# Layer 1 of a graph network on Trainium2: the scan's silus side by side, exponential and logarithm from one table set, and fewer, wider products

## The chip, the cores and the metric

The kernel runs on one core of one Trainium2 chip. The metric is the device time of one execution in microseconds (us); lower is better. The core has a matrix engine (PE, with PEld for its weight loads), a vector engine (DVE), a scalar engine (ACT) that evaluates functions such as exponential or silu from tables that it loads, a general engine (POOL) and SP, which issues transfers. Each engine works through its own instructions in a fixed order, and waits where data made by another engine is missing.

## The reference, cut to what matters

A network of two layers on `x` of shape (32, 512, 256) with an adjacency `adj` of shape (32, 512, 512). Each layer is a graph step and a feed-forward step on normalized rows, each added to `x`. The change lies in layer 1, whose feed-forward step compresses each batch of 512 rows into 64 "slice" tokens, runs a two-way state-space scan (`_hydra`) over these, and expands again:

```
z, xBC, dt = split(u @ in_w.T)                  # z 512, x 512, B 64, C 64, dt 8 + 8 columns
dt  = softplus(dt + dt_bias)                    # one half forward, one half backward
xBC = silu(causal_conv(xBC, width 3) + conv_b)  # -> x, B, C
dA  = exp(dt * -exp(A_log))
y   = scan(dA, dt, B, x; C), forward + backward
y   = y + x * (x @ fcD_w.T + D)
yg  = y * silu(z)
return (yg * rsqrt(mean(yg**2) + 1e-5) * norm_w) @ out_w.T
```

The graph step of layer 1 is an attention over 4 heads whose weights are masked by `adj`.

## The kernel before

`tile_kernel` runs `layer0_sorted` and then `layer1_plain` (a fallback behind `tc.If` does not run here). The start of layer 1 (its constants, its weights turned by PE) is woven into the end of layer 0. The program is written as generators, and a scheduler then fixes the order of the instructions on each engine; each engine keeps that order.

In `layer1_plain` the 32 batches pass two streams. `attentions` runs `prepare(b)`, `attention(b)` and `norm(b)` for one batch after another. `mixer(g)` takes two batches (`GB = 2`) through `slices` (twice), `tokens`, `scan` and `unslice` (twice); so there are 16 scans. The main loop advances the attention stream by credits while it draws from `mixer`, so that attention work for later batches fills the engines during a scan.

In `prepare`, rows of `x` are gathered by POOL (L1142, indirect transfers), normalized (`normed`: DVE statistics, POOL power, ACT L1121), transposed into `x3T`, and multiplied by the head weights (`hp`, L1171); ACT evaluates three small exponentials of each product (L1174 to L1176) and copies the rest to `ht` (L1177). A Square of the mask with an accumulated sum (L1164) counts its entries; its elementwise result is not needed, and it is written into `ht` before the copies come. A row `mine` is turned, written to DRAM (`ownd`, L1188) and read back to all partitions (`own`, L1191); the attention weights `att` (L1204) need it. `add_rows` (L947) lets POOL's queue add a constant row to `x` by an accumulating transfer.

`scan(g, uT)` works on 128 rows, 64 tokens of each of two batches. In its order:

- `xp` (L1394): x in columns, 16 products; `bcp` (L1403): B and C one after the other, each 64 partitions wide, both on partitions 0 to 63.
- `dtp` (L1422): step sizes laid out for forward and backward in 16 small products, and once more in rows (L1387 with 16 columns).
- the softplus of the step sizes: DVE rows, an exponential (L1431) and a logarithm (L1437).
- `zp` (L1387, 512 columns) and its silu (L1444); convolutions of x (L1411, L1413) and their four silus (L1449); the convolutions of B and of C and their silus (L1456).
- `la`, `seg` (L1475), `gp` (L1481), `segp` (L1485), the exponential `decay` (L1487), `xtp`, `qp`, and the DVE rows `mix` (L1502 to L1504).
- `yp` (L1511): 16 products of 64x64, eight on the upper half of the array for the first batch, then eight on the lower half for the second.
- `y`, its transpose `yTp`, its mean square `ms` (L1524), `oTp` (L1529), `msp` (L1537, four products that spread `ms`), `rms`, `vp` (L1551).

ACT holds one table set at a time. Where the next function is not in it, a load stands before the instruction: in a scan before L1449 (twice), L1431, L1437, L1444 and L1487. PSUM tiles come from one pool (`psum`), each of one bank.

Of the kernel before, what the change touches and what calls it, by code (L numbers as in the profile page):

```python
# [8 lines left out]
F32 = mybir.dt.float32  # L9
# [10 lines left out]
P = 128  # L20
# [844 lines left out]
def layer1_plain(tc, ident, eps, x2s, ranks, adj, w, out, over, ps):  # L865
# [6 lines left out]
    GB = 2  # L872
# [28 lines left out]
    with ExitStack() as ctx:  # L901
# [55 lines left out]
        nc.vector.tensor_scalar_mul(bfx_eps, bfx[:, :, 0], -1e-5)  # L957
        conv_w = const("conv_w", [P, KC, KW], w["hy_conv_w"][:DI].rearrange("(c p) k -> p c k", p=P))
        conv_b = const("conv_b", [P, KC], w["hy_conv_b"][:DI].rearrange("(c p) -> p c", p=P))
        bc_w = const("bc_w", [S, 2, KW], w["hy_conv_w"][DI:].rearrange("(c p) k -> p c k", p=S))  # L960
        bc_b = const("bc_b", [S, 2], w["hy_conv_b"][DI:].rearrange("(c p) -> p c", p=S))
        skip = const("skip", [P, H], w["hy_D"].partition_broadcast(P))
        dtb = ctile("dtb", [P, 4, H])
        for i in range(4):
            nc.sync.dma_start(dtb[:, i, :], w["hy_dt_bias"].partition_broadcast(P))
        nega = const("nega", [P, H], w["hy_A_log"].partition_broadcast(P))
        nc.scalar.activation(nega, nega, AF.Exp)
# [29 lines left out]
        with tc.tile_pool(name="raw", bufs=2, side="right") as raw:  # L997
# [4 lines left out]
            for i in range(2):  # L1002
# [4 lines left out]
            nc.sync.dma_start(bs, w["b_slice"].rearrange("(o n) -> o n", o=1))  # L1007


            pieces = [(dst, w[name], r0)  # L1010
                      for dst, name in ((wfxT, "W_fx"), (inT, "hy_in_w"), (hoT, "hy_out_w"), (owT, "out_w"),
                                        (fcT, "hy_fcD_w"))
                      for r0 in range(0, w[name].shape[0], P)]

            def fetch(i):

# [89 lines left out]

        xs, ready, attended, stored = {}, {}, set(), set()

        def normed(xt, xn, name):

            mv = sb.tile([P, NT, 2], F32, tag="mv" + name[0], name=f"mv{name}")
            for t in range(NT):
                st = sb.tile([P, 6], F32, tag="st" + name[0], name=f"st{name}_{t}", bufs=4)
                nc.vector.bn_stats(st, xt[:, t, :])
                nc.vector.bn_aggr(mv[:, t, :], st)
            rs = sb.tile([P, NT], F32, tag="rs" + name[0], name=f"rs{name}")
            deviation(nc, rs, mv[:, :, 1], eps)
            shift = sb.tile([P, NT], F32, tag="shift" + name[0], name=f"shift{name}")
            nc.vector.scalar_tensor_tensor(shift, mv[:, :, 0], -1.0, rs, ALU.mult, ALU.mult)
            for t in range(NT):  # L1120
                nc.scalar.activation(xn[:, t, :], xt[:, t, :], AF.Identity, bias=shift[:, t : t + 1],  # L1121
                                     scale=rs[:, t : t + 1])
# [13 lines left out]
        def prepare(b):  # L1136
# [12 lines left out]
            if b:  # L1149
# [11 lines left out]


            ht = sb.tile([P, NT, AH * HO], F32, tag="ht", name=f"ht{b}")
            nc.scalar.activation(ht.rearrange("p t e -> p (t e)").bitcast(BF16), mask.rearrange("p t n -> p (t n)"),  # L1164
                                 AF.Square, bias=centre, accum_out=edges[:, b : b + 1])
            other = sb.tile([P, NT, AH], F32, tag="other", name=f"other{b}")
            mine = sb.tile([P, AH, NT], F32, tag="mine", name=f"mine{b}")
            for t in range(NT):
                ph = psum("any", f"hp{b}_{t}")
                for c in range(DC):  # L1170
                    nc.tensor.matmul(ph[:, : AH * (HO + 2)], xnT[:, c, t * P : (t + 1) * P], wa[:, c, :],  # L1171
                                     start=c == 0, stop=c == DC - 1)
                d = ph[:, AH * HO : AH * HO + AH]
                nc.scalar.activation(mine[:, :, t], ph[:, AH * (HO + 1) : AH * (HO + 2)], AF.Exp, scale=1.0 - SLOPE)  # L1174
                nc.scalar.activation(hv[:, t, :, HO], d, AF.Exp)
                nc.scalar.activation(other[:, t, :], d, AF.Exp, scale=SLOPE - 1.0)  # L1176
                nc.scalar.copy(ht[:, t, :], ph[:, : AH * HO])  # L1177
                yield

            nc.gpsimd.tensor_add(hv[:, :, :, :HO], ht.rearrange("p t (h e) -> p t h e", h=AH),  # L1180
                                 abias.rearrange("p (h e) -> p h e", h=AH).unsqueeze(1).to_broadcast([P, NT, AH, HO]))
# [195 lines left out]
        def scan(g, uT):  # L1377
# [13 lines left out]
            px = psum("any", f"xp{g}")  # L1391
            for k in range(KC):
                for c in range(KC):
                    nc.tensor.matmul(px[:, k * T : (k + 1) * T], inT[:, c, DI + k * P : DI + (k + 1) * P],  # L1394
                                     uT[:, c, :], start=c == 0, stop=c == KC - 1)
            xpad = sb.tile([P, KC, GB, LP], F32, tag="xpad", name=f"xpad{g}", bufs=1)
            nc.gpsimd.memset(xpad[:, :, :, : KW - 1], 0.0)
            nc.scalar.copy(xpad[:, :, :, KW - 1 :], px.rearrange("p (k j l) -> p k j l", k=KC, j=GB))
            pb = psum("any", f"bcp{g}")
            for i in range(2):  # L1400
                c0 = 2 * DI + i * S
                for c in range(KC):
                    nc.tensor.matmul(pb[:S, i * T : (i + 1) * T], inT[:, c, c0 : c0 + S], uT[:, c, :],  # L1403
                                     start=c == 0, stop=c == KC - 1)
            bpad = sb.tile([S, 2, GB, LP], F32, tag="bpad", name=f"bpad{g}", bufs=1)
            nc.gpsimd.memset(bpad[:, :, :, : KW - 1], 0.0)
            nc.scalar.copy(bpad[:, :, :, KW - 1 :],
                           pb[:S, : 2 * T].rearrange("p (k j l) -> p k j l", k=2, j=GB))

            def conv(src, wts, dst):  # L1410
                nc.vector.tensor_scalar_mul(dst, src[:, :, 0:G], wts[:, 0:1])  # L1411
# [3 lines left out]

            pd = psum("any", f"dtp{g}")
            for j in range(GB):
                for i in range(2):  # L1420
                    for c in range(KC):
                        nc.tensor.matmul(pd[i * G : (i + 1) * G, j * H : (j + 1) * H],  # L1422
                                         uT[:, c, j * G : (j + 1) * G],
                                         inT[:, c, DT0 + i * H : DT0 + (i + 1) * H],
                                         start=c == 0, stop=c == KC - 1)
            tok_matmul(pd[:, 2 * H : 4 * H], DT0, 2 * H)
            sp = sb.tile([P, 5, 4 * H], F32, tag="sp", name=f"sp{g}")
            v, e, u, r, dt = (sp[:, i, :] for i in range(5))
            nc.vector.tensor_add(v, pd[:, : 4 * H], dtb.rearrange("p i h -> p (i h)"))
            nc.vector.scalar_tensor_tensor(e, v, -1.0, v, ALU.mult, ALU.min)  # L1430
            nc.scalar.activation(e, e, AF.Exp)  # L1431

            nc.vector.tensor_scalar_add(u, e, 1.0)
            nc.vector.reciprocal(r, u)
            nc.vector.scalar_tensor_tensor(e, u, -1.0, e, ALU.add, ALU.subtract)
            nc.vector.tensor_mul(e, e, r)
            nc.scalar.activation(u, u, AF.Ln)  # L1437
            nc.vector.tensor_sub(u, u, e)
            nc.vector.scalar_tensor_tensor(dt, v, 0.0, u, ALU.max, ALU.add)

            pz = psum("any", f"zp{g}")
            tok_matmul(pz, 0, DI)
            z = sb.tile([P, DI], F32, tag="z", name=f"z{g}", bufs=1)
            nc.scalar.activation(z, pz, AF.Silu)  # L1444
            xT = inner(f"xT{g}")
            for k in range(KC):
                dst = chunks(xT)[:, k, :]
                conv(xpad[:, k], conv_w[:, k, :], dst.rearrange("p (j l) -> p j l", j=GB))
                nc.scalar.activation(dst, dst, AF.Silu, bias=conv_b[:, k : k + 1])  # L1449
            bcT = sb.tile([S, 2, GB, G], F32, tag="bcT", name=f"bcT{g}", bufs=1)  # L1450
            cpad = sb.tile([S, GB, G + 2], F32, tag="cpad", name=f"cpad{g}", bufs=1)
            nc.gpsimd.memset(cpad[:, :, 0 : G + 2 : G + 1], 0.0)
            for i in range(2):
                conv(bpad[:, i], bc_w[:, i, :], bcT[:, i])
                dst = bcT[:, 0] if i == 0 else cpad[:, :, 1 : G + 1]
                nc.scalar.activation(dst, bcT[:, i], AF.Silu, bias=bc_b[:, i : i + 1])  # L1456

            la = sb.tile([P, GB, H], F32, tag="la", name=f"la{g}")  # L1460
            nc.vector.tensor_mul(la, dt[:, : GB * H].rearrange("p (j h) -> p j h", j=GB),
# [14 lines left out]
            yield 7  # L1476

            pg = psum("any", f"gp{g}")
            for j in range(GB):
                for i in range(2):  # L1480
                    nc.tensor.matmul(pg[j * G : (j + 1) * G, i * G : (i + 1) * G], bcT[:, 0, j, :],  # L1481
                                     cpad[:, j, 2 * i : 2 * i + G], start=True, stop=True)
            pl = psum("any", f"segp{g}")
            for j in reversed(range(GB)):
# [20 lines left out]

            yield 7
            py = psum("any", f"yp{g}")
            for j in range(GB):
                half = slice(j * G, (j + 1) * G)
                for h in range(H):  # L1510
                    nc.tensor.matmul(py[half, h * C : (h + 1) * C], heads(mix)[half, h, :],  # L1511
                                     heads(xk)[half, h, :], start=True, stop=True)
            y = inner(f"y{g}")
# [17 lines left out]
            oT = inner(f"oT{g}")  # L1531
            nc.scalar.copy(oT, po)

            pm = psum("any", f"msp{g}")
            for j in range(GB):
                for i in range(P // C):
                    nc.tensor.matmul(pm[i * G : (i + 1) * G, j : j + 1], ident[:, j * G : (j + 1) * G], ms,  # L1537
                                     start=True, stop=True)
            rms = sb.tile([P, GB], F32, tag="rms", name=f"rms{g}")
            nc.vector.tensor_scalar(rms, pm[:, :GB], 1.0 / DI, LN_EPS, ALU.mult, ALU.add)  # L1540
            nc.gpsimd.tensor_tensor(rms, rms, eps[:, 1:2].to_broadcast([P, GB]), ALU.pow)
            yield 2

# [689 lines left out]
```

## Time and profile before

| what | value |
|---|---|
| three runs | 4292.98, 4299.84, 4306.08 us; median 4299.84 |
| the profiled execution | 4311.61 us; span 4309.8 us |
| busy, whole span | PE 3825.7, PEld 2426.9, DVE 3170.3, ACT 2188.1, POOL 1584.8 us |
| 3500 to 3700 us, in layer 1 | PE 190.19, DVE 145.06, ACT 97.92, POOL 57.66 of 200 us |
| granted PE clock | 0.949 over the span; 0.98 to 1.00 from 2500 to 4100 us |
| first and last `xpad` copy of a scan | 2522.5 and 4247.1 us |
| ACT table loads in the 16 scans | 96, of 1283 ns each |

Busy times are sums over the span, so a share says nothing of which wait ends last at a given place; for that, one reads the chain of waits and the timelines of one stretch. Scans recur every 111 to 118 us between 2519 and 4140 us. The last two have no or little attention work beside them: between 4139.7 and 4241.7 us PE idles 10.5 us, in the 69.3 us after it 13.6 us, and in each of the groups before 3.2 to 6.7 us.

### The profile page before, as it was taken

The page shows a single profiled execution, that of the slowest core. Times are in us where ns is not written, and L with a number is a line of the kernel's source. Part 1 is how long each engine was busy: PE and PEld are TensorE (multiplying, and loading weights), DVE is VectorE, ACT ScalarE, POOL GpSimd, SP SyncE. Part 2 cuts the span into 40 slices and gives each one's busy share as a digit, 9 for nine tenths or more (in the row PEclk, how much of TensorE's full clock was granted, in tenths as well). Part 3 has the DMA queues.
Part 4 walks back from the last instruction along what each step waited for, and adds up shares of the span by engine and source line. Part 5 has one row for each costly group of instructions (what it writes and reads, how often), then busy time and mean ns, then how long its engine had stood idle before and what let it go on. Part 6 is the DMA issues. An engine that isn't in the chain of part 4 may idle for free.

```text
span 4309.8 us, 56063 instructions
## 1 busy us (share of the span) xinstructions
PE 3825.7 (89%) x19799; PEld 2426.9 (56%) x19799; DVE 3170.3 (74%) x6909; ACT 2188.1 (51%) x4308; POOL 1584.8 (37%) x1973
## 2 busy tenths in 40 slices
PE   5567998989989999888999799999999999999997
PEld 4454565565655656555555355555555555555655
DVE  6668887898778987777776677767777776777763
ACT  3344655566555665555665344454444444444533
POOL 2345643565435644355331322222222223322210
PEclk8778999999999999998999899999999999999998
DMA  4547654575445754377552432333233333232210
GB/s 128 162 154 225 199 164 135 174 231 165 150 127 179 227 163 141 111 248 194 152 157 56 97 70 70 72 74 69 69 79 74 79 79 78 65 74 65 59 30 16
DMA packets 313536, 524.04 MB, mean 122 GB/s; under 512 B 104823, under 2 KB 196611, under 8 KB 313244
## 3 DMA queue, kind: packets, MB, share of 16 engines
q0 software_dynamic: 129408, 383.06, 32.0%
q1 hardware_dynamic: 183836, 137.30, 11.0%
q8 instruction: 158, 2.59, 0.2%
q14 instruction: 134, 1.10, 0.1%
HBM read 463.11 MB, written 73.95 MB: 125 GB/s over the span
## 4 chain that ended last, share of the span: by engine, by line
PE 43%; DVE 21%; DMA 10%; issue 8%; POOL 6%; ACT 4%; DVEq 0%; SPq 0%; POOLq 0%; ACTq 0%
PE clsp L623 5%; PE gatep L623 5%; PE po L652 5%; PE yTp L1341 4%; PE avp L1241 3%; DVE att L1204 3%; PE lgp L1329 3%; DVE acc L637 2%; DMA rows<-table,xs 2%; DVE best L599 2%; DMA best<-table,xs 2%; PE adp L1246 2%; DMA x<-x2s,ranks 1%; PE xp L1394 1%; PE hp L1171 1%
## 5 line engine op out<-in xcount | busy, mean ns | idle before, releaser
L623 PE MATMUL clsp<-xnT,wc 128*128 128x512 f32 x1024 | 523.4, 630 | 47.6 <-ACT cls L625 40.8
L623 PE MATMUL gatep<-xnT,wg 128*128 128x512 f32 x1024 | 496.1, 604 | 14.2 <-ACT gate L625 13.6
L652 PE MATMUL po<-wd,acc 128*128 128x256 f32 x2048 | 453.0, 380 | 4.9 <-DVE acc L641 4.0
L652 PEld LDWEIGHTS po<-wd,acc 128*128 128x128 f32 x2048 | 387.1, 190 | 72.6 <-issue 10.8
L1204 DVE SCALAR_TENSOR_TENSOR att<-own,other,mask 128x512 f32<-128x512 f32 x512 | 365.2, 741 | 57.0 <-DMA own<-ownd 56.9
L599 DVE SCALAR_TENSOR_TENSOR best<-rows,xs,best 128x1024 f32<-128x1024 f32 x212 | 271.1, 1281 | 134.3 <-ACT best L593 81.5
L637 DVE SCALAR_TENSOR_TENSOR acc<-past,fld,acc 128x512 f32<-128x512 f32 x448 | 332.6, 745 | 30.6 <-ACT past L636 22.8
L623 PEld LDWEIGHTS gatep<-xnT,wg 128*128 128x128 f32 x1024 | 195.9, 195 | 253.9 <-issue 199.9
L632 ACT ACTIVATE acc<-tz,fld 128x512 f32<-128x512 f32 x256 | 199.0, 778 | 265.5 <-PE tz L630 235.4
L596 POOL DMA_INDIRECT rows<-table,xs x212 | 258.5, 1219 | 204.3 <-DVE best L599 136.8
L636 ACT ACTIVATE past<-tz,fld 128x512 f32<-128x512 f32 x448 | 291.1, 694 | 80.1 <-DVE acc L637 79.7
L623 PEld LDWEIGHTS clsp<-xnT,wc 128*128 128x128 f32 x1024 | 184.3, 201 | 185.1 <-issue 114.7
L1241 PE MATMUL avp<-att,hv 128*32 128x512 f32 x2048 | 257.3, 605 | 30.8 <-DVE att L1204 30.8
L435 PE MATMUL pm<-h,adj 128*128 128x258 f32 (+1 forms) x1024 | 179.6, 322 | 100.5 <-DVE keep L428 39.0
L1341 PE MATMUL yTp<-sw,x 128*128 128x512 f32 x512 | 239.0, 609 | 32.0 <-DVE sw L1336 22.6
L1142 POOL DMA_INDIRECT x<-x2s,ranks x128 | 151.0, 1179 | 309.7 <-DVE x L1563 138.1
L625 ACT ACTIVATE gate<-gatep,fld 128x512 f32<-128x512 f32 x256 | 175.8, 687 | 161.6 <-PE gatep L623 132.6
L1329 PE MATMUL lgp<-wsl,x4T 128*128 128x512 f32 x512 | 244.9, 620 | 13.1 <-ACT x4T L1131 7.2
L1294 POOL TENSOR_TENSOR mu<-mu,eps 128x16 f32<-128x16 f32 x32 | 115.4, 3606 | 371.0 <-DVE mu L1293 371.0
L554 POOL DMA_INDIRECT xs<-rows_of,order x128 | 156.4, 1222 | 253.3 <-DVE acc L637 100.3
L1561 PE MATMUL outp<-v,swT 128*128 128x256 f32 x1024 | 227.4, 380 | 0.0
L435 PEld LDWEIGHTS pm<-h,adj 128*128 128x128 f32 x1024 | 150.2, 211 | 125.8 <-issue 71.3
(585 smaller groups left out, 8393.6 us busy)
## 6 DMA issues: line engine op xcount, KB each, us to landing
adj<-in_adj POOLq DMA_DIRECT2D x128, 256.0 KB
x<-added POOLq DMA_DIRECT2D x64, 512.0 KB
own<-ownd SPq DMA_DIRECT2D x128, 256.0 KB
rows_of<-keep SPq DMA_DIRECT2D x32, 550.0 KB
x<-in_x SPq DMA_DIRECT2D x32, 512.0 KB
xs<-bd POOLq DMA_DIRECT2D x32, 512.0 KB
x2s<-xs SPq DMA_DIRECT2D x32, 512.0 KB
short<-in_adj POOLq DMA_DIRECT2D x32, 512.0 KB
```

The costliest lines, as they stand in the source:

```text
L435: nc.tensor.matmul(pm[:, : c1 - c0], a[:, i, t * P : (t + 1) * P], h[:, i, c0:c1], start=i + c0 == 0, stop=i + 1 == NT and c0 > 0)
L596: nc.gpsimd.indirect_dma_start(out=row, out_offset=None, in_=table, in_offset=bass.IndirectOffsetOnAxis(ap=idxs[:, k : k + 1].bitcast(U32) ...
L599: nc.vector.scalar_tensor_tensor(m, row, vals[:, k : k + 1], m, ALU.add, ALU.max)
L623: nc.tensor.matmul(pf, wf[:, c, f * P : (f + 1) * P], xnT[:, c, :], start=c == 0, stop=c == DC - 1)
L636: nc.scalar.activation(r, z, AF.Relu, bias=fld[:, f, AT + b : AT + b + 1])
L637: nc.vector.scalar_tensor_tensor(y, r, fld[:, f, CH + b : CH + b + 1], y, ALU.mult, ALU.add)
L652: nc.tensor.matmul(po[:, i, :], acc[f][:, t * P : (t + 1) * P], wd[:, f, :], start=f == 0, stop=f == FC - 1)
L1204: nc.vector.scalar_tensor_tensor(e, own[h], other[:, j, h : h + 1], mask[:, j, :], ALU.max, ALU.mult)
L1241: nc.tensor.matmul(pv[p][k * HW : (k + 1) * HW, :], hv[:, j, h, e : e + HW], weighed[b, h, j], **ends)
L1329: nc.tensor.matmul(pf, xnT[:, c, t * P : (t + 1) * P], wsl[:, c, :], start=c == 0, stop=c == DC - 1)
L1341: nc.tensor.matmul(py, xn[:, t, c * P : (c + 1) * P], sw[:, t, :], start=t == 0, stop=t == NT - 1)
L1561: nc.tensor.matmul(po[:, :D], swT[:, k, t * P : (t + 1) * P], v[:, k, :], start=k == 0, stop=k == KC - 1)
```

## The change

It does these things in `layer1_plain`:

- The columns of `in_w` are stored with the 16 step-size columns first, so that they lie beside z. `z` is computed as two products: step sizes with the first half of z (272 columns, into the bank `pb` of B and C), and the second half (256 columns, bank `pz`).
- B and C become one product, one convolution on 128 partitions; the silu of C moves it from partitions 64 to 127 to partitions 0 to 63.
- The small products of the step sizes are gone; five DVE additions arrange the halves from the rows.
- All silus come together; then one set that holds exponential and logarithm is loaded explicitly, and the exponential, the logarithm (and later `decay`) are ordered behind it (`behind`, `tc.issue_after`).
- `gp` and `yp` alternate between the two batches, product by product.
- `msp` is gone; four DVE instructions on 64 partitions spread `ms`.
- The Square of the mask is written into `xnT` (`x3T`), after the `hp` products, no longer into `ht` before them.

```diff
-            nc.scalar.activation(ht.rearrange("p t e -> p (t e)").bitcast(BF16), mask.rearrange("p t n -> p (t n)"),
-                                 AF.Square, bias=centre, accum_out=edges[:, b : b + 1])
...
+            nc.scalar.activation(xnT.rearrange("p c n -> p (c n)").bitcast(BF16), mask.rearrange("p t n -> p (t n)"),
+                                 AF.Square, bias=centre, accum_out=edges[:, b : b + 1])
...
+            pb, pz = psum("any", f"bcp{g}"), psum("any", f"zp{g}")
+            for c in range(KC):
+                nc.tensor.matmul(pb[:, :T], inT[:, c, DIN - P :], uT[:, c, :], start=c == 0, stop=c == KC - 1)
+            first = 2 * H + DI // 2
+            tok_matmul(pb[:, T : T + first], 0, first)
+            tok_matmul(pz[:, : DI // 2], first, DI // 2)
...
+            nc.vector.tensor_add(v[:, 2 * H :], pd, dtb.rearrange("p i h -> p (i h)"))
+            for i in range(2):
+                for j in range(GB):
+                    half = slice(j * G, (j + 1) * G)
+                    nc.vector.tensor_add(v[i * G : (i + 1) * G, j * H : (j + 1) * H],
+                                         pd[half, i * H : (i + 1) * H], dtb[half, 0, :])
...
+            silus.append(nc.scalar.activation(z[:, : DI // 2], pb[:, T + 2 * H : T + first], AF.Silu))
+            silus.append(nc.scalar.activation(z[:, DI // 2 :], pz[:, : DI // 2], AF.Silu))
...
+            conv(bpad, bc_w, bcT)
+            for half, dst in ((slice(0, S), bcT[:S]), (slice(S, P), cpad[:, :, 1 : G + 1])):
+                silus.append(nc.scalar.activation(dst, bcT[half], AF.Silu, bias=bc_b[half]))
+            xT = inner(f"xT{g}")
+            for k in range(KC):
+                dst = chunks(xT)[:, k, :]
+                conv(xpad[:, k], conv_w[:, k, :], dst.rearrange("p (j l) -> p j l", j=GB))
+                silus.append(nc.scalar.activation(dst, dst, AF.Silu, bias=conv_b[:, k : k + 1]))
...
+            both = nc.scalar.preload_act_table_set("natural_log_exp_and_others")
+            for silu in silus:
+                behind(both, silu)
+            with tc.issue_after(both.ins):
+                nc.scalar.activation(e, e, AF.Exp)
...
+            with tc.issue_after(both.ins):
+                nc.scalar.activation(u, u, AF.Ln)
...
-            for j in range(GB):
-                half = slice(j * G, (j + 1) * G)
-                for h in range(H):
+            for h in range(H):
+                for j in range(GB):
+                    half = slice(j * G, (j + 1) * G)
                     nc.tensor.matmul(py[half, h * C : (h + 1) * C], heads(mix)[half, h, :],
                                      heads(xk)[half, h, :], start=True, stop=True)
...
-                    nc.tensor.matmul(pm[i * G : (i + 1) * G, j : j + 1], ident[:, j * G : (j + 1) * G], ms,
-                                     start=True, stop=True)
+                    nc.vector.tensor_scalar(rms[i * G : (i + 1) * G, j : j + 1], ms[j * G : (j + 1) * G], 1.0 / DI, LN_EPS,
+                                            ALU.mult, ALU.add)
```

and the new helper, which orders one instruction behind another on the same engine without a semaphore:

```python
        def behind(ins, other):
            order = mybir.DependencyInfo(mybir.DependencyClass.NoSync, mybir.DependencyReason.DATA)
            tc.add_manual_dep(ins.ins, other.ins.name, order, reason="tables")
```

Two constants shrink with it: `dtb` is filled by two transfers, not four, and the weights of B's and C's convolution are loaded as one block of 128 partitions.

## The prediction

> **What bounds the kernel now.** I read the busy table first (PE 3825.7 us of 4309.8, DVE 3170.3), then the stretches: in layer 1, from 2500 to 4100 us, every 200 us hold 188 to 193 us of PE and only 140 to 149 us of DVE. So PE looks like the bound of the stage that the change touches. Then the chain of waits over one mixer group (two batches, one scan), 3560 to 3680 us; its period, from one `xp` to the next, is 117.0 us, of which PE idles 6.5 us. The columns are start, time, engine and line:
>
> ```profile
> 3562.40 3.77 PE xp L1394 x32
> 3566.17 1.89 PE bcp L1403 x16
> 3568.06 1.20 PE dtp L1422 x32
> 3569.26 0.99 PE dtp L1387 x8
> 3570.25 3.53 PE zp L1387 x8
> ...
> 3579.94 0.39 PE gp L1481 x8
> 3580.32 1.01 PE segp L1485 x4
> ...
> 3590.86 0.26 ACT turned L1186
> 3591.14 6.04 DMA ownd<-turned
> 3597.19 3.31 DMA own<-ownd
> ...
> 3608.65 3.44 DMA out<-x
> ```
>
> The reader is to see two regimes. From `xp` to `segp` the chain is PE without a gap. From `turned` to the softmax products `yTp` (3636.8) it is not PE at all: a row goes to DRAM and back (9.35 us), DVE makes attention weights and adds `x`, `x` is stored, the next `x` is gathered, POOL raises to a power, DVE scales `sw`. A PE saving is kept only in the first regime, and there only if ACT and DVE could have been ready earlier. How ready they were is in the timelines of ACT, of DVE and of PE (start, length, what, and in brackets the idle time before it and its releaser):
>
> ```profile
> 3573.78 1.28 ACT L1437 ACT_TABLE_LOAD   x1
> 3575.13 0.23 ACT L1437 ACTIVATE sp<-sp 128x32 f32<-128x32 f32 x1
> ```
>
> ```profile
> 3568.81 0.48 DVE L1411 TENSOR_SCALAR xT<-xpad,conv_w 128x128 f32<-128x128 f32 x2
> ...
> 3577.94 0.16 DVE L1119 SCALAR_TENSOR_TENSOR shiftd<-mvd,rsd 128x4 f32<-128x4 f32 x1 [1.41 <-POOL rsd L31]
> ```
>
> ```profile
> 3586.19 1.87 PE L1511 MATMUL yp<-xk,mix 64*64 64x64 f32 x32 [0.71 <-DVE mix L1504]
> ...
> 3595.53 3.67 PE L1551 MATMUL vp<-owT,oT 64*64 64x256 f32 x32 [0.34 <-ACT oT L1532]
> ```
>
> DVE reaches the convolutions only at 3568.81, 2 us after `xpad` stood ready, because it first finishes the norm of the batch before; `seg` was ready at 3579.97, 0.3 us before PE came to `segp`. DVE was as late as PE.
>
> **PE work, from start-to-start distances** (x32 is 16 matmuls, two records each). Removed: `bcp` 1.79, the halves of `dtp` 1.29, `dtp` in rows 0.92, `zp` 3.51: 7.51 us. Added: 4 of 128x128 at 3.77/16 = 0.236: 0.94; 4 of 272 columns at 0.46 (`hp`, 264 columns, leaves two every 0.89 us): 1.83; 4 of 256 columns at 0.438 (`outp`: 16 in 7.01): 1.75. Sum 4.52, so 2.99 less. `msp` frees 0.40, but `vp` behind it waits for the copy `oT` anyway: 0.
>
> For `yp` in turns, row and rule differ. The row is `vp`: two 64x64 tiles in turns, 16 matmuls of 256 columns in 3.60 us, 0.225 each, half of `outp`'s 0.438. So `yp` falls from 1.80 to 0.90 us. The Trainium skill ("TensorEngine Tiling (Array Packing)", section Restrictions and Gotchas) says that different row tiles cannot access one PSUM bank at once; `py` is one bank and its two halves are different row tiles, so by the rule `yp` stays at 1.80 (+0.9 us a group on my sum). `vp` writes its halves into one bank too, so I take the row. `gp`, in turns over column strips like `avp`, falls from 0.38 to about 0.2. In all PE has 4.1 us less a group (4.5 with `msp`), 72 us over 16 groups if all were kept.
>
> **ACT: six table loads become two** (the built order shows one before the first silu, one behind the last), 4 x 1.283 = 5.1 us a group. The skill ("ScalarE: Activation LUTs", section What ACT_TABLE_LOAD costs) gives 1.283 us and a drain of 1.38 us, which would make it 10.6 us; the trace agrees on the load and shows no drain (3575.13 follows 3573.78 by 1.35), so 5.1. On the path it is worth little: the old loads ran beside PE's 17.5 us. What is new on the path is the order: exponential, `seg` and `segp` now stand behind all silus.
>
> **Timetable of this group after the change**, by the built order and the durations above. DVE is unchanged to 3568.81. Four convolutions (0.75 each) 3571.85, one `att` 0.66, five step-size adds (0.1 apart; four are new, cross-partition, not in the trace: between 0.06 and 0.19 each, the spacing and the length of `sp` rows; I take 0.1) 3573.0; `bcT` with two batch-norm rows between, 3574.7. It is one convolution of 128 partitions instead of two, 0.75 less. Silus of B and C to 3575.4, load to 3576.7, exponential 3576.95; DVE has waited for `rsd` (1.41) meanwhile. Logarithm behind two `x` rows on ACT, 3578.4; sub, `dt`, `la` 0.22 each, `seg` 1.29: 3580.4. So `segp` starts **0.1 us later** than now (3580.32). PE, earlier by 2.9, waits 1 us for `gp` (the silu of C) and 2 us for `seg`. Its saving is gone here, and with it the cover of the exponential: each us there now costs one.
>
> From `segp` to `yp` nothing changes (`dq` waits for `qp`, then five DVE rows of 0.6): `yp` 3586.3. `yp` halved: y done 0.8 us earlier. But the **Square of the mask** (2.00 us, L1164) moves. Now it stands at the head of `ht`, where it made ACT wait (62.5 us over 27 times, `mu` L1292) and once a group kept exponentials of `sw` behind it (3622.83); PE waited 1.52 us for that. In the new order it follows the fourth `hp` copy, ahead of `yT` and `turned`: copy ends 3588.75, Square 3590.75, `yT` 3591.4. So `oTp` and `vp` come **0.45 later** than now, `turned` 1.2 later. In the second batch it delays two `x4T` copies by 0.5. Queued behind it on ACT are `yT`, the square of y, `turned`; PE waits for the first, DVE through `own` for the last.
>
> Against it: `hv` and `x` (L1121) now run on ACT before `decay`, at 3577 to 3581.4, not 3586 to 3589. POOL's two `x<-added` transfers, 512 KB each, wait for them and start some 7 us earlier. Now they fill the DMA engines from 3588 to 3594.6 (96% busy in 3590 to 3595), in front of `ownd`, which takes 6.05 us; in the second batch, with nothing before it, 1.39. The first batches of the 14 groups lie between 3.1 and 6.1, mostly near 4. After the change: 3592.4 + 1.4 + 3.3 = 3597.1 against 3600.53. DVE's sum of `x` then waits for `outp`, not for `own`: it ends 3607.0 instead of 3608.54, and store, gather, power and `sw` follow 1.5 earlier. In the next group it is 1.1. Minus 0.5 for `x4T`: **about 1.0 us a group gained**. Bounds: 0.5 lost (where `ownd` was fast already) to 3 gained (groups 2 and 3, where `lgp` waits 2.7 us behind the Square).
>
> The last two groups have little attention to fill with. In the last, PE waits 4.36 for `gp`, 3.48 for `yp`; `seg` comes about 2.3 earlier with fewer loads and `yp`, 3.28 there at the lower clock, halves: 4. The one before: `yp` halves, 2. The rest: two SP transfers fewer at the start, beside layer 0's PE, 0; piece order of `inT`, same ten pieces, 0; three small DVE rows for `rms`, 0.3 us beside `oTp`, 0.
>
> **Sum**: 14 x 1.0 + 2 + 4 = 20 us. The profiled execution took 4311.6 (span 4309.8), so 4291.6 like for like; it lies 11.8 over the median 4299.84, so **4280** as a median.
>
> **Rivals.** *PE keeps its saving* (0.16): the DVE chain had slack that I don't see, and the count of PE decides: 14 x 4.4 + 6 = 68, 4232. For it: PE at 95%. Against: `seg` 0.3 us ahead of PE.
> *The silus hold the exponential* (0.21, slower): one mechanism, at L1431. If the convolution of B and C ends later than 3574.7, everything to `segp` shifts by as much, with no cover. The adds at 0.19, a dependent convolution row of 0.34 and one more `att` ahead make 1.5 to 2.5. At 2.5, each group loses 1.5: 14 x 1.5 - 4 = +17, 4317. It decides from 1 us on.
> *The transfers are not relieved* (0.17): `ownd` stays slow beside the transposed mask (3574.4) or the write's own landing; then only the later `turned` is left, +1.3: 14 x 1.3 - 6 = +12, 4312.
> As worked (0.46): 4262 to 4296.
>
> What this kernel can tell from no change is 0.3%, 13 us: below 4287 is faster, above 4313 slower. Faster: 0.40 of the first case and all of the PE rival, 0.56; slower 0.14 of the silu rival and 0.05 of the transfers, 0.19; same 0.25. Leaving out the ends of both rivals, 4236 to 4314.
>
> **What would show it.** Table loads in layer 1 from 96 to 32; `yp` near 0.9 us (right) or 1.8; PE waiting about 1 for `gp` and 2 for `segp` in each group (if neither, the PE rival holds; if over 4, the silu rival); `ownd` to `own` 1.4 in first batches; Square 2.0 just ahead of `yT`, `oTp` waiting over 1.5. I am wrong if PE's idle time a group falls below 6.5, or if the period grows.

## The result and the profile after

The change makes no difference: 14 runs of each gave 4304.39 us (4286.51 to 4310.56) against 4303.49 (4291.78 to 4314.58); the ratio of after to before is 1.0007, 95% interval 0.9993 to 1.002. The forecast was 20 us less. The profiled execution took 4294.7 us (span 4293.0), but it entered the first scan at 2498.9 us, before's at 2518.7. That is layer 0 and not the change: in the 15 profiled executions of this document the first scan begins anywhere between 2496 and 2526 us. From the first scan to the end of the span it is 1791.1 us before and 1794.1 after. So single profiles are compared here by the distance from one `xp` to the next (the period of a group), and kernels by their ratio. A period is of one execution, and a difference of half a us between two says little: three kernels below that differ only in what fills one wait have 115.07, 115.50 and 115.58.

| mean of groups 0 to 13, us behind `xp` | before | after | change |
|---|---|---|---|
| `segp` | 17.65 | 18.29 | +0.64 |
| `yp` | 23.61 | 24.04 | +0.43 |
| `oTp` | 28.43 | 29.39 | +0.96 |
| `vp` | 32.94 | 34.95 | +2.01 |
| next `xp` (the period) | 115.79 | 116.39 | +0.60 |

14 groups lose 8.4 us together, group 14 gains 3.6, the last 1.8. PE is busy 53.5 us less (3772.2 for 3825.7) and ACT 83.1 less (2105.0 for 2188.1), and neither shows in the time.

The timeline of PE in group 9 after (its `xp` starts at 3548.38; columns: start, length, what, and in brackets the idle time before it and its releaser):

```profile
3561.73 0.45 PE L1491 MATMUL gp<-cpad,bcT 64*64 64x64 f32 x8 [1.47 <-ACT cpad L1445]
3562.11 1.92 PE L1248 MATMUL avp<-att,hv 128*32 128x512 f32 x16
3563.85 1.04 PE L1253 MATMUL adp<-att,hv 128*32 128x512 f32 x8
3566.72 1.08 PE L1495 MATMUL segp<-seg,seg_l 128*64 128x512 f32 x4 [1.83 <-DVE seg L1485]
```

```profile
3572.66 1.15 PE L1521 MATMUL yp<-xk,mix 64*64 64x64 f32 x32 [0.71 <-ACT ht L1182]
3573.74 1.16 PE L1176 MATMUL hp<-wa,x3T 128*128 128x264 f32 x4
3575.41 0.63 PE L1531 MATMUL yTp<-ident,y 128*128 128x128 f32 x4 [0.51 <-DVE y L1526]
3575.87 0.27 PE L1191 MATMUL minep<-ident,mine 128*16 128x128 f32 x1
3578.02 5.46 PE L1539 MATMUL oTp<-yT,hoT 128*128 128x128 f32 x32 [1.88 <-ACT yT L1533]
3584.16 2.16 PE L1559 MATMUL vp<-owT,oT 64*64 64x256 f32 x18 [0.68 <-ACT oT L1542]
```

PE waits 1.47 for `gp`, 1.83 for `segp` and 1.88 for `oTp`. In the same group of before it waited for neither of the first two, and 0.62 for `oTp`. `yp` is short (1.08 from its start to that of `hp`). New is the 5.46 of `oTp`; in before the same sixteen products took 3.84:

```profile
3591.01 3.84 PE L1529 MATMUL oTp<-yT,hoT 128*128 128x128 f32 x32 [0.62 <-ACT yT L1523]
```

The next view, the stretches of group 9, shows why (after, columns: stretch, its length, busy time of PE, PEld, DVE, ACT and POOL, the granted clock, DMA share, GB/s):

```profile
3574.00:3576.00 2.00, 1.49 (x9) 0.89 (x8) 1.23 (x2) 1.06 (x5) 0.41 (x1) 1.00 0.00 0
3576.00:3578.00 2.00, 0.14 (x2) 0.00 (x0) 0.04 (x1) 2.00 (x4) 1.93 (x1) 1.00 0.00 0
3578.00:3580.00 2.00, 1.98 (x13) 1.98 (x14) 1.90 (x8) 0.69 (x3) 0.00 (x0) 0.72 0.02 4
3580.00:3582.00 2.00, 2.00 (x11) 2.00 (x11) 0.00 (x0) 0.00 (x0) 0.71 (x1) 0.50 0.26 86
3582.00:3584.00 2.00, 1.48 (x12) 1.29 (x11) 0.54 (x1) 0.48 (x1) 0.00 (x0) 0.92 0.95 314
```

PE stands nearly still for 2 us, then starts at full clock and is cut to half for 3.4 us (the clock records of the trace come in pieces of 3.413 us). Group 7 of the same execution has the same waits and no cut, so the length of the wait alone does not decide. What differs is where it falls. From the first scan on, the 19 low stretches of after all begin on one grid of 3.413 us, to within 1 ns, and this grid lies differently to the program in each execution. One piece of it in group 9, then the three around the start of `oTp` (3348.01) in group 7:

```profile
3575.48:3578.89 3.41, 1.53 (x12) 1.25 (x13) 0.93 (x3) 3.21 (x7) 2.34 (x1) 1.00 0.00 0
3343.37:3346.78 3.41, 2.26 (x24) 1.45 (x20) 1.38 (x2) 1.85 (x5) 1.20 (x1) 1.00 0.03 5
3346.78:3350.20 3.42, 2.19 (x19) 2.19 (x20) 1.93 (x8) 1.90 (x6) 1.33 (x2) 1.00 0.01 2
3350.20:3353.61 3.41, 2.73 (x25) 2.21 (x26) 0.29 (x1) 0.92 (x2) 0.52 (x1) 1.00 0.67 204
```

In group 9 PE idles 1.88 of 3.41 us in one piece, and the next runs at half clock. In group 7 a border of the grid divides the wait, 1.15 and 1.23 us are idle in two pieces, and the clock stays. Nine of the 14 groups are cut (0, 3, 6 and 8 to 13); the piece before the cut holds 1.86 to 2.38 us of idle in them, and in the other five no piece there holds more than 1.50, but for group 2 with 1.86. From `oTp` to `vp` it is 6.14 us in the cut ones, and 4.51 in the other five and in all 14 of before (where no piece holds more than 1.13).

What PE waits for is in the timeline of ACT, same group:

```profile
3575.11 0.39 ACT L1182 COPY ht<-hp 128x256 f32<-128x256 f32 x1
3575.36 2.03 ACT L1184 ACTIVATE x3T<-mask,centre 128x2048 bf16<-128x2048 bf16 x1
3577.27 0.22 ACT L1184 ACTIVATION_READ_ACCUMULATOR x3T<-mask,centre 128x1 f32 x1
3577.36 0.60 ACT L1533 COPY yT<-yTp 128x512 f32<-128x512 f32 x1
```

The Square stands just ahead of `yT`, as the built order had said. The chain of waits now runs from it through `yT`, `oTp`, `vp` and `outp` to DVE's sum of `x`, so the low clock of `oTp` lies on it.

### The profile page after: what moved, and what is told of

Read it like the earlier page. It is cut to its first block, busy times and chain, and to the rows that moved or that the text cites. A ratio compares the mean times of both kernels' runs of the same rounds, so it can differ in the third digit from the quotient of the medians.

```text
span 4293.0 us, 54585 instructions
## 1 busy us (share of the span) xinstructions
PE 3772.2 (88%) x19031; PEld 2392.6 (56%) x19031; DVE 3183.1 (74%) x6973; ACT 2105.0 (49%) x4260; POOL 1576.3 (37%) x1973
```

## Experiments

The questions were: does the low clock cost the time, or only go with it; what in the wait brings it; is the Square's new place the cause; and what is the rest worth, the grouping of tables, the order of softplus and silus, the turns of `yp`. Kernels that ran together share their runs of before. "Period" is the mean of groups 0 to 13 in the one profiled execution, "cut" the number of these groups in which `oTp` ran at the low clock there.

| run | differs from | ratio to before (95%) | period | cut |
|---|---|---|---|---|
| after | | 1.0007 (0.9993 to 1.002) | 116.39 | 9 |
| warm2 | after | 0.9972 (0.9959 to 0.9985) | 115.58 | 0 |
| warm1 | after | 0.9967 (0.9953 to 0.9981) | 115.07 | 0 |
| warm_tr | after | 0.9958 (0.9943 to 0.9974) | 115.50 | 0 |
| sq_turn | after | 0.9970 (0.9958 to 0.9982) | 115.30 | 0 |
| sq_old | after | 0.9960 (0.9947 to 0.9972) | 115.16 | 0 |
| b_sq | before | 1.0009 (0.9996 to 1.0022) | 116.37 | 7 |
| exp_first | sq_old | 0.9927 (0.9909 to 0.9944) | 114.58 | 0 |
| exp_turn | sq_turn | 0.9896 (0.9879 to 0.9914) | 113.59 | 0 |
| exp_new | after | 0.9936 (0.9915 to 0.9958) | 114.85 | 8 |
| no_group | sq_old | 1.0133 (1.0117 to 1.0149) | 119.41 | 4 |
| b_tab | before | 0.9981 (0.9966 to 0.9997) | 115.38 | 0 |
| b_yp | before | 0.9997 (0.9986 to 1.0008) | 115.65 | 0 |
| et_yp | exp_turn | 0.9896 (0.9872 to 0.9920) | 114.06 | 0 |

### The low clock: warm2, warm1, warm_tr

```diff
             po = psum("any", f"oTp{g}")
+            for _ in range(2):      # warm1: range(1)
+                nc.tensor.matmul(po, ident, y, start=True, stop=True)
```

In warm_tr the line is `nc.tensor.transpose` of one 128-column block of `y` into a block of `po`, eight times. What they write, `oTp` overwrites.

> After, plus two matmuls of 128x512 into oTp's bank while PE waits for yT; oTp overwrites what they wrote. Theory A (clock gate): in 9 of 14 groups oTp (16 products) runs at a granted clock of 0.5 and takes 5.46 us instead of 3.84, because PE idles just before it. With PE busy there, oTp starts as late as in after (29.4 us behind xp) but oTp to vp falls from 5.56 to 4.5 in all groups, the period by about 1.0, the time by 10 to 16 us. Theory B (oTp is long for another reason, e.g. PE's operands or ACT's copy oT; or the chain downstream absorbs it): oTp to vp stays near 5.5, or it falls and the period stays at 116.4: time unchanged within 4 us.

> As warm2, with one extra product instead of two: PE's wait for yT (1.88 us in after, 0.15 in warm2) is filled to about half, some 1.0 us remain. If the low clock depends on how much of a stretch PE idles: no group, or few, with the low clock; oTp (extra product counted in) to vp near 5.5 in all groups, oTp starting 0.85 later than in warm2; time within 5 us of warm2. If any wait of a microsecond at this place brings it: groups with 1.6 us more, as in after, and the time near after's.

> As warm1, but PE's wait for yT is filled by eight transposes of 128x128 (by the spacing of yTp 0.12 us each, some 1.0 us) instead of one ordinary product of 1.02 us. Theory A (any work of PE keeps the clock): as warm1, no group with the low clock, oTp proper to vp 4.5, ratio to before 0.996 to 0.998. Theory B (transposes do not count as work: in after the low clock follows 3.12 us without an ordinary product, from the end of hp to oTp, in which yTp and minep, transposes both, ran): the low clock stays in 6 to 11 of 14 groups, and the time is that of after (1.000 to 1.002).

The timeline of PE in group 9 of warm1, and then of warm_tr:

```profile
3566.44 1.02 PE L1539 MATMUL oTp<-y,ident 128*128 128x512 f32 x2
3568.47 3.84 PE L1542 MATMUL oTp<-yT,hoT 128*128 128x128 f32 x32 [1.01 <-ACT yT L1534]
3572.98 2.38 PE L1562 MATMUL vp<-owT,oT 64*64 64x256 f32 x20 [0.68 <-ACT oT L1545]
```

```profile
3598.40 1.04 PE L1539 MATMUL oTp<-ident,y 128*128 128x128 f32 x8
3600.44 3.84 PE L1542 MATMUL oTp<-yT,hoT 128*128 128x128 f32 x32 [1.00 <-ACT yT L1534]
```

`oTp` proper starts no earlier in group 9 than in after (29.65 us behind `xp` in both, 29.64 there) and takes 3.84 again; no group is cut. Work was added to PE, the traces show all other instructions of PE, ACT, DVE and POOL in the order of after, and the ratio fell by 0.0035, 0.0040 and 0.0049 from that of after, 15 to 21 us of 4300. Nine times 1.63 would be 14.7; up to 4.6 us more come from the last group (66.3 us in after, 65.9, 62.7 and 61.7 here). Theory A of warm2 holds: the low clock costs the time. Of warm1's two readings the first holds: half of the wait filled is enough. No piece of the grid before `oTp` then holds more than 1.52 us of idle, so the missing cuts are no luck of the grid. And warm_tr tells that it is PE's standing still: transposes keep the clock as products do.

### The Square's place: sq_turn, sq_old, b_sq

```diff
-            nc.scalar.copy(row, pt[: AH * NT, :P])
+            turned_row = nc.scalar.copy(row, pt[: AH * NT, :P])
+            square = nc.scalar.activation(xnT.rearrange("p c n -> p (c n)").bitcast(BF16),
+                                          mask.rearrange("p t n -> p (t n)"),
+                                          AF.Square, bias=centre, accum_out=edges[:, b : b + 1])
+            behind(square, turned_row)
```

That is sq_turn, with the Square taken from its place in after. sq_old puts it where it was in before; b_sq is before with that one line moved as the change moves it.

> After, with the Square ordered behind the copy of the turned row, so no longer ahead of yT. Theory A (the Square's place costs twice: 0.5 us of wait and the low clock that this wait brings): yp to oTp falls from 5.35 to about 3.5 to 4, oTp to vp from 5.56 to 4.5, vp about 33 us behind xp, ownd issued 1.2 to 2 us earlier; 1.5 to 2 us a group, 20 to 30 us in all: 4274 to 4284 beside 4304 of after. Rival C (the end of a group is set by the attention chain, not by oTp): vp comes earlier but the period falls by less than 0.5; time within 7 us of after.

> After, with the Square back in its old place (into ht, ahead of the head products); all else as in after. If the new place of the Square is what spoilt the change: oTp to vp 4.5 and vp about 33 us behind xp as in sq_turn, but the waits of lgp and mu behind the Square (1 to 2.7 us a group in before) are back: 5 to 15 us under after. If the old place costs as much as the new one: within 5 us of after.

> Before, with only the Square moved (into the transposed rows, behind the head products). If the Square's new place alone brings the late yT and the low clock: yp to oTp over 5.2 and oTp to vp over 5 in most groups, against 4.82 and 4.51 in before; time 5 to 12 us over before, less what lgp no longer waits (1 us a group). If the low clock comes only from the joint effect with a shorter yp and PE's new waits for gp and segp: oTp to vp stays 4.5, the time 0 to 10 us under before.

The line of `oTp` in group 9 of sq_turn, then of b_sq:

```profile
3580.37 3.84 PE L1541 MATMUL oTp<-yT,hoT 128*128 128x128 f32 x32 [0.56 <-ACT yT L1535]
3577.02 5.39 PE L1529 MATMUL oTp<-yT,hoT 128*128 128x128 f32 x32 [1.87 <-ACT yT L1523]
```

Out of its new place, by either way, the Square no longer holds `yT`: `oTp` waits 0.56 us, `oTp` to `vp` is 4.51 in groups 0 to 13, and 16 (sq_turn) and 20 us (sq_old) are won against after. (The scheduler also set other rows of ACT and DVE in a new order in both, so the gain is not the Square's alone.) For sq_turn that is theory A in kind and less than its 20 to 30 us; rival C falls, as the period fell by 1.09. sq_old gained more than expected: waits of `lgp` behind it came back in two groups (2.92 and 4.06 us), not in most. b_sq shows that nothing else of the change is needed: before with the Square moved waits 1.88 at `oTp` and is cut in 7 groups. Its time is not told from before's. Its groups are 0.58 longer in the profile, 8 us in all, which the interval (2 us less to 9 more) allows; the waits for `lgp` (11.3 us over groups 0 to 13 of before) went with the move, but that they pay for the cuts is not shown.

With `segp` at the same place, the period of groups 9 and 10 can be set against `vp`: at 32.86 us (sq_old, sq_turn) it is 114.7 to 114.9, at 34.2 (warm1, warm2, warm_tr) 114.1 to 114.4, at 35.8 (after) 115.9 and 115.95. In these two groups the wait alone, 1.3 us, costs nothing that shows, and the 1.6 of the low clock, which come on top, cost all of 1.6. This is a hint and no proof: each is one execution, and warm2 has 115.7 in groups 7 and 8 without a cut.

### Softplus and silus: exp_first, exp_turn, exp_new, no_group, b_tab

```diff
+            nc.scalar.activation(e, e, AF.Exp)
...
+            ln = nc.scalar.activation(u, u, AF.Ln)
...
             silus = []
...
             both = nc.scalar.preload_act_table_set("natural_log_exp_and_others")
             for silu in silus:
+                behind(silu, ln)
                 behind(both, silu)
-            with tc.issue_after(both.ins):
-                nc.scalar.activation(e, e, AF.Exp)
...
-            with tc.issue_after(both.ins):
-                nc.scalar.activation(u, u, AF.Ln)
```

In exp_first softplus stands in the program ahead of the silus (the diff against sq_old, cut), with the Square in before's place; exp_turn has the Square behind the turned row, exp_new where the change has it. no_group is sq_old with no order between softplus and silus and no explicit load; b_tab is before with exponential and logarithm behind all silus, as in the change, and nothing else.

> As sq_old (after with the Square in its old place), but exponential and logarithm stand ahead of the silus, on the set that is still loaded; the silus are ordered behind the logarithm, the set for exponential and logarithm is loaded again behind the last silu: still two loads a scan. Theory A (the price that ate PE's saving is the place of the exponential: it stood ready 3.4 us and waited for the silus and a load): the wait for seg (1.83 us) and most of that for gp (1.48) go, segp starts 15 to 15.5 us behind xp instead of 18.3, vp near 30; as the gathers meet the next mask's transfer, a third to a half of it is kept: 1 to 1.5 us a group, 14 to 20 us under sq_old. Rival B (the end of a group is set by the attention chain on DVE, POOL and DMA): segp comes earlier, but yp and the period keep their times within 0.4 us; time within 6 us of sq_old.

> As exp_first, with the Square behind the turned row. In after, the same move and the move back to the old place gave nearly the same time (4286.7 and 4285.4). If that holds here too: within 5 us of exp_first. If exp_first makes lgp wait behind the old Square, as before did in five of 14 groups (1 to 2.7 us): 5 to 15 us under exp_first.

> As exp_turn (softplus ahead of the silus), with the Square in the place that the change gave it, ahead of yT. It fills the two by two with after, sq_turn and exp_turn. If the Square's place costs by its wait and by the low clock here too: oTp waits about 1.9 us, oTp to vp 6.1 in half of the groups or more, 10 to 20 us over exp_turn. If the low clock in after needed the waits for gp and seg as well: oTp to vp 4.5 and 3 to 8 us over exp_turn.

> As sq_old, without the grouping of tables: exponential and logarithm in the place and with the loads of before (six loads a scan, about 5.1 us more of ACT). Theory A (the grouping itself costs on the path, since the exponential waits for all silus): segp 1 to 2 us earlier than in sq_old, the time 5 to 15 us under sq_old. Rival B (the loads removed pay for the order): segp as late as in sq_old or later, by up to 2 us, and the last two groups 2 to 4 us longer; time 0 to 20 us over sq_old.

> Before, with the grouping of tables alone: exponential and logarithm behind all silus, loads from six to two a scan; products, Square and yp as in before. Theory A (the loads removed are what the change gains, as taking the grouping out of sq_old cost 71 us): segp no later than in before and 10 to 40 us faster, the last two groups by 2 us each. Rival B (the six loads hurt only with the merged products, where all silus come at once; in before they lay beside PE): segp 0.5 to 2 us later than before's 17.65, since the exponential now waits for the silu of C; 0 to 25 us slower.

First what after does, in the timelines of DVE (first line) and ACT, group 9:

```profile
3559.41 0.18 DVE L1434 SCALAR_TENSOR_TENSOR sp<-sp 128x32 f32<-128x32 f32 x1
```

```profile
3561.28 0.40 ACT L1445 ACTIVATE cpad<-bcT,bc_b 64x128 f32<-64x128 f32 x1
3561.70 1.28 ACT L1455 ACT_TABLE_LOAD   x1
3562.99 0.23 ACT L1459 ACTIVATE sp<-sp 128x32 f32<-128x32 f32 x1
3563.38 1.10 ACT L1128 ACTIVATE x<-x,shiftd,rsd 128x256 f32<-128x256 f32 x2 [0.16 <-DVE shiftd L1126]
3564.38 0.21 ACT L1466 ACTIVATE sp<-sp 128x32 f32<-128x32 f32 x1
```

The exponential's operand is done at 3559.59 and stands 3.40 us, behind the silu of C and a load of 1.28; the logarithm then stands behind two `x` rows. The same stretch of exp_turn (its `xp` at 3538.97), ACT and then PE:

```profile
3548.51 0.23 ACT L1437 ACTIVATE sp<-sp 128x32 f32<-128x32 f32 x1 [2.67 <-DVE sp L1436]
3548.65 0.56 ACT L1138 COPY x3T<-x3T22p 128x512 f32<-128x512 f32 x1
3549.69 0.23 ACT L1443 ACTIVATE sp<-sp 128x32 f32<-128x32 f32 x1 [0.48 <-DVE sp L1441]
3549.94 1.28 ACT L1450 ACT_TABLE_LOAD   x1
3551.24 0.38 ACT L1450 ACTIVATE z<-bcp 128x256 f32<-128x256 f32 x1
```

```profile
3552.64 0.45 PE L1493 MATMUL gp<-cpad,bcT 64*64 64x64 f32 x8 [0.48 <-ACT cpad L1457]
3553.01 1.04 PE L1250 MATMUL avp<-att,hv 128*32 128x512 f32 x2
3553.99 1.08 PE L1497 MATMUL segp<-seg,seg_l 128*64 128x512 f32 x4
```

Here it is ACT that waits for the operand, not the reverse. PE comes to `segp` at 15.02 us without a wait, 3.3 earlier than in after, with the same two loads a scan. Not all of that reaches `yp`: it is 1.0 earlier in exp_first than in sq_old, and 2.3 in exp_turn than in sq_turn. exp_first is 0.0033 below sq_old (14 us, the low end of theory A; its period fell by 0.58 and not by 1 to 1.5, and 5 us came in group 14), exp_turn 0.0074 below sq_turn (32 us): **exp_turn beats both kernels, by 1.0%**. The old place of the Square is worse once the rest is faster (`lgp` waits 3.09 and 3.60 in groups 2 and 3 of exp_first): exp_turn is 13 us under exp_first (six runs of each, and the intervals overlap a little). exp_new, 0.0040 over exp_turn, fills the square: `oTp` waits 1.86 in most groups and 8 are cut (17 us): the first reading. The wait for `seg` is gone there, and 1.07 of that for `gp` is left in the mean; that the cut needs neither is shown by b_sq, which has none of the two.

no_group is far outside what was expected, 74 us over sq_old: rival B has the sign, but it went to 20. Silu, exponential, silu, logarithm, silu and `decay` alternate there, a load before each; PE waits 3.8 us for `gp`, and the mean granted clock from 2500 to 4100 us is 0.96 (0.99 in sq_old, 1.00 in before). How the 74 us divide between these was not tried. b_tab is 8 us faster than before (the interval just clear of none), short of theory A's 10. `segp` was 0.16 later, and PE waited 0.61 for it; the gain is 5.7 us over groups 0 to 13 and as much in group 14, where `yp` waits 1.02 instead of 4.71. So the grouping is worth 8 us in before and 74 with the merged products. That it is so because these let all silus come at once is argued from the order in no_group, not shown by a run.

### The turns of yp: b_yp, et_yp

```diff
-            for j in range(GB):
-                half = slice(j * G, (j + 1) * G)
-                for h in range(H):
+            for h in range(H):
+                for j in range(GB):
+                    half = slice(j * G, (j + 1) * G)
```

> Before, with only the order of yp's products changed (the two batches in turns). By the row of vp, yp falls from 1.87 us busy to about 1.0 to 1.15. Theory A (the saving is kept, since PE and the row sent to DRAM both follow yp): 0.8 us in each of 16 groups: 10 to 14 us under before. Rival B (the row's slow write, not yp, sets the end): time within 4 us of before. If different row tiles of one bank were serialized: yp stays at 1.87 and the time at that of before.

> As exp_turn, with yp's products in the order of before. In before the turns were worth 1.6 us in all (not told from none), since the end of a group did not follow yp there. If PE leads to vp in exp_turn: the eight and eight cost 0.6 to 0.8 us a group, 8 to 13 us over exp_turn. If the attention chain sets the end here as well: within 4 us of exp_turn.

In before the turns are worth nothing that can be told (0.9997): `oTp` comes 0.49 earlier, and the period follows by 0.14 (rival B). In exp_turn the old order has `vp` 0.72 later and the same ratio; the expected 8 to 13 us did not come, though with six runs of each the intervals cannot exclude 8 us, and the period of the one profile is 0.47 longer.

## Why the prediction failed, by its steps

- **The step that failed** is "So `oTp` and `vp` come **0.45 later** than now". `oTp` came 0.96 later (29.64 in group 9 for the forecast 29.1), of which 0.41 stood already at `segp`. But between `oTp` and `vp` the prediction took before's 4.51 for granted, and it became 6.14 in nine groups: the wait in front of `oTp` brings the low clock, a term that it put at nothing. The term is 1.05 us a group, 15 us in all by its own length, and 15 to 21 us by the three runs that took it away. With it removed and all else kept, the change is 0.28 to 0.42% faster, 12 to 18 us, where 20 was forecast. Before's own profile held the warning, and the prediction used it for `yp` alone ("3.28 there at the lower clock"): in groups 14 and 15, where PE waits most, `oTp` to `vp` is 7.21 and 5.89. I saw a new wait of 1.3 us and priced only the wait.
- **The sum "14 x 1.0"** took one group for all, and this failed too. Group 9 did fall by 1.03 (116.98 to 115.95), but that it met the forecast was luck: 1.52 of `lgp` wait had gone, which only eight of the groups had (11.3 us in all), and 1.6 of low clock had come. Over the 14 groups a gain of 14 us was forecast and a loss of 8.4 measured; 14.7 of the difference is the low clock by its own length. Without the cuts the mean period falls by 0.21 (warm2), 0.29 (warm_tr) or 0.72 (warm1), not by 1.0. So the 12 to 18 us of the kernels without cuts come near the forecast in part because the last two groups gain 6 to 10 in them.
- **Silus, load, exponential: right in time.** Times behind `xp` in group 9: the exponential is done at 14.84 (forecast 14.6), the logarithm at 16.21 (16.1), and `segp` begins at 18.34 (18.1). PE waits 1.47 and 1.83, where 1 and 2 were forecast. The silu rival was to decide from 1 us on; it stayed below, +0.64 in the mean, of which 0.23 is group 0 alone (+3.26). Yet its place was the right one to look at: what PE saved was lost there, and turning the order round brings 32 us.
- **PE work, `yp`: right in kind.** `yp` takes 1.08, where 0.90 was forecast; the row of `vp` held, and the rule on row tiles that share a bank, which would have left 1.80, did not. `gp` stayed at 0.38 (forecast 0.2), with no effect, as PE waited in front of it. All of PE's saving was to vanish in waits, and did.
- **Table loads: right.** 32 loads in the 16 scans, 1283 ns each, followed by the next row after 1.29: no drain, as the row said. "Worth little on the path" held in before (8 us by b_tab), not for the merged products (no_group).
- **Transfers: right.** From the issue of `ownd` to that of `own`, 1.36 (3578.71, 3580.07), for 1.4 forecast (1.34 to 1.38 in ten of the 14 groups, 1.68 to 3.50 in the other four); the first `att`, which `own` releases, began 35.08 behind `xp` (34.8). It was not kept, because `outp` then came last, as forecast, but too late (DVE waits 3.59 for it): DVE's sum of `x` ended 47.0 behind `xp` instead of the forecast 44.7, and 2.1 of the difference is `vp` (35.78 for the forecast 33.65).
- **Last groups:** -3.6 and -1.8, forecast -2 and -4; the sum was right.
- **Its signs:** those that it named for its mechanism came (the fast transfer in ten of 14 groups), and so did one of its two signs of being wrong: the period grew.

## What to carry to other kernels

Where a change puts a wait of 1 to 2 us in front of a run of products, add up PE's idle time within 3.4 us there, the waits just before included, and price the products at the low clock too, as one outcome among several; a few products or transposes into a bank about to be overwritten are a cheap test. When functions of two table sets are grouped, ask which group the critical value is in: that one goes first, on the set that is still loaded. And work the timetable for more than one group, one with the waits of the others, before it is multiplied by their number.

## What the runs showed of the hardware

- The granted clock changes in pieces of 3.413 us on a fixed grid, and what counts is how long PE idles within one piece. In groups 0 to 13 of all 15 traces, every full-clock piece with 2.1 us of idle or more was followed by one at half clock (65 of 65), and none with less than 1.6 was (some 6800); in between, 40 of 106 were. That is a count over kernels, not an experiment on the wait's length.
- So a pause of 1.88 us, with one of 0.51 before it and 0.73 of transposes between, is cut or not by its place on the grid. An estimate from these lengths: if 1.83 us of idle are enough, 63% of the places are bad, if 1.9 are needed, 37%. The runs had 9, 7 and 8 of 14 (after, b_sq, exp_new), and another execution can have another number. With the second pause at 1.0 (warm1, warm_tr) the two make 1.5, and none of 28 groups was cut. The Trainium skill ("TensorE: Matmul & The Clock Gate", section What's actually happening) gives at least one idle window of some 3.4 us for the low clock; here little more than half of one was enough, and the measurement decides.
- The same page ("Part 4: PE-mode transpose") says that transposes do not count as PE work in the same way. In warm_tr eight of them kept the clock as well as one product of the same length.
